# Two samples per count matmul: the second sample's one-hot rows scaled by 256, and the counts evicted as 16-bit integers

## The chip, the core and the metric

The kernel runs on one core of a Trainium2 chip. The metric is the device time of one execution in microseconds (us). Below, PE is TensorE's matmul unit, DVE is VectorE, ACT is ScalarE, POOL is GpSimd and SP is SyncE.

## What is computed

The reference is the forward pass of a recommender model for 16384 samples:

```
tok = word_emb[token_idx].mean(axis=1)      # 32 rows of 300, of 50000
e1, e2, e3 = mean of 20 rows each of emb_mh1, emb_mh2, emb_mh3   # rows of 64
o1..o4 = one row each of emb_oh1..emb_oh4
emb = concatenate([tok, e1, e2, e3, o1, o2, o3, o4], axis=1)     # 748 columns
wide = the same lookups, summed, in tables that are one column wide
h = relu(emb @ W1 + b1); h = relu(h @ W2 + b2); h = relu(h @ W3 + b3)
return sigmoid(h @ Wd + bd + wide)
```

W1 is 748 x 1024, W2 is 1024 x 512, W3 is 512 x 256.

## The kernel before

Samples are taken in 128 tiles of 128. Each tile has two kinds of lookups.

**Large table.** The 32 token rows of each sample are gathered from the chip's main memory: `tokens()` issues one indirect DMA on POOL's queue for each of the 32 index columns (L255), 128 rows of 1200 bytes each, two of them to a buffer `tok_rows`, with 8 buffers (`TOK_BUFS`). There are 4096 such gathers. DVE adds the rows up in `add_up` (L237, L239, L243). A gather waits until the adds have read its buffer.

**Small tables.** The seven small tables lie in SBUF as bf16, three terms that sum up to the f32 value (`terms`, made by `convert_tables`), cut into `n_h` = 138 slices of 128 rows. A lookup is made by counting: for each sample a 128 x 138 matrix says how often row l of slice h is asked for. `one_hots` (L314) compares the 64 lookup keys of each sample, which lie on 64 partitions, with an iota, and so makes `row1` (which of 128 rows) and `slice1` (which of 138 slices) in bf16; the upper 64 partitions hold the keys of a second sample. `counts` (L330) multiplies the two: one matmul over 64 partitions for each sample, with `f` choosing the lower or the upper half of the partitions, 12 matmuls of 64 x 138 for six pairs of samples, into a PSUM tile `pc` of four banks of which there is one. ACT evicts it into `cnt` as fp8, scaled by 0.5 (L347). One tile of samples takes 11 such steps (`STEPS`; the last has four pairs), so there are 1408 steps. During the next tile `small_sums` (L355) multiplies the counts, as weights (128 x 128, fp8), with the table terms (195 columns of bf16): 138 matmuls `pg` for each tile, and DVE reduces each pair of results (L371).

**Layers.** For two tiles at a time `mlp` runs the three layers in f32 (L461), each result evicted by ACT with Relu (L470) from one of two PSUM buffers `ph`.

**Order.** The order of all instructions is written out by the loop at L570 (`manual_schedule`). A step issues, in this order: the one-hots of the next step (DVE), the counts of this step (PE, then ACT), table conversions at the start of the run, transposes, token gathers and adds up to a share of the whole that grows evenly with the steps, the `pg` matmuls of this step, and layer matmuls up to an even share. The 16 last steps (`WAKE`) have no counts. Each engine takes its instructions in this order. Near the end `early_part` begins the last block's first layer in the tile of `pc`.

The line that matters for the layout of the counts is the eviction at L347: `cnt` is `[P, 2, HALF, n_h]`, so the 138 slices of a sample lie next to each other, and the weight load of `by_slice[:, :, h]` reads every 138th byte.

Of the kernel before, what the change touches and what calls it, by code (L numbers as in the profile page):

```python
# [11 lines left out]
I32 = mybir.dt.int32  # L12
U32 = mybir.dt.uint32
AF = mybir.ActivationFunctionType
ALU = mybir.AluOpType
AX = mybir.AxisListType

P = 128
# [10 lines left out]
LAYER_TILES = 2  # L29
HALF = P // 2  # L30
N_SMALL = 3 * N_MH + 4
ONEHOT = 6
# [19 lines left out]
def kernel(  # L52
# [46 lines left out]
    ps_h = ctx.enter_context(tc.tile_pool(name="ps_h", bufs=2, space=bass.MemoryType.PSUM))  # L99
    ps_c = ctx.enter_context(tc.tile_pool(name="ps_c", bufs=1, space=bass.MemoryType.PSUM))  # L100
    ps_g = ctx.enter_context(tc.tile_pool(name="ps_g", bufs=1, space=bass.MemoryType.PSUM))
# [45 lines left out]
    terms = const.tile([P, n_h, 3 * ROW], BF16, name="terms")  # L147
    minus_half = const.tile([P, P], BF16, name="minus_half")
    nc.vector.tensor_single_scalar(minus_half, ident, -0.5, op=ALU.mult)

# [16 lines left out]
    def convert_tables():  # L167
# [19 lines left out]
        def make(p, c):  # L187

            if c == 0:
                nc.scalar.activation(term(p, 0), rows(p), AF.Copy, scale=2.0)  # L190
                return
            _, a, b = pieces[p]
            left = ps_h.tile([P, SPLIT, ROW], F32, name="left", tag="ph")[:, 0 : b - a, :]
            nc.tensor.matmul(left, ident, rows(p), start=True, stop=False)  # L194
            for k in range(c):
                nc.tensor.matmul(left, minus_half, term(p, k), start=False, stop=(k == c - 1))
            nc.scalar.activation(term(p, c), left, AF.Copy, scale=2.0)

# [67 lines left out]
    def load_indices(blk):  # L266


        b0 = blk * BLOCK
        it = idxp.tile([P, NSUB, N_TOK], I32, name="it")  # L270
        nc.sync.dma_start(
            out=it, in_=idx[b0 : b0 + BLOCK, 0:N_TOK].rearrange("(s p) c -> p s c", p=P)
        )
        ix = keyp.tile([P, NSUB // 2, 2, N_SMALL], I32, name="ix")
        for s in range(NSUB):
            nc.sync.dma_start(
                out=ix[(s % 2) * HALF : (s % 2 + 1) * HALF, s // 2],
                in_=idx[b0 + s * P : b0 + (s + 1) * P, IDX_MH:IDX_COLS].rearrange(
                    "(f p) c -> p f c", p=HALF
                ),  # L280
            )
        token_indices[blk] = it
        return ix
# [30 lines left out]
    def one_hots(sc, s, i):  # L314
# [5 lines left out]
        for w, (one, n) in enumerate(((row1, P), (slice1, n_h))):  # L320
            shape = [P, rows, n // 2, 2]
            nc.vector.tensor_tensor(  # L322
                one[:, 0:rows, :].rearrange("p i (n d) -> p i n d", d=2),
                iota[:, 0:n].rearrange("p (n d) -> p n d", d=2).unsqueeze(1).to_broadcast(shape),
                sc[:, s // 2, w, s % 2, b : b + rows, :].unsqueeze(2).to_broadcast(shape),
                ALU.is_equal,
            )
        return row1, slice1

    def counts(cnt, hot, i):  # L330
# [3 lines left out]
        n = rows // 2  # L334
        pc = ps_c.tile([P, 2, 2, 512], F32, name="pc")
        for k in range(rows):
            for f in range(2):
                half = slice(f * HALF, (f + 1) * HALF)
                at = k % n * n_h
                nc.tensor.matmul(  # L340
                    pc[:, f, k // n, at : at + n_h],
                    hot[0][half, k, :],
                    hot[1][half, k, :],
                    start=True,
                    stop=True,
                )
        nc.scalar.activation(  # L347
            cnt[:, :, b : b + rows, :].rearrange("l f (g k) h -> l f g (k h)", g=2),
            pc[:, :, :, 0 : n * n_h],
            AF.Copy,  # L350
            scale=0.5,
            saturate=False,
        )

    def small_sums(g, cnt):  # L355


        by_slice = cnt.rearrange("l f p h -> l (f p) h")
        for i in (0, 2, 4, 6):
            pair = SMALL[i : i + 2]  # L360
            pg = ps_g.tile([P, 2, 3 * ROW], F32, name="pg")
            for j, f in enumerate(pair):
                h0, h1 = slices[f]
                for h in range(h0, h1):
                    nc.tensor.matmul(  # L365
                        pg[:, j, :], by_slice[:, :, h], terms[:, h, :], start=(h == h0), stop=(h == h1 - 1)
                    )
# [69 lines left out]
    def early_part(block):  # L437


        part = ps_c.tile([P, 4, 512], F32, name="pc")  # L440
        for m in range(4):
            for k in range(NK - 3):
                nc.tensor.matmul(
                    part[:, m, 0 : block.n],
                    w1_sb[: chunk_k[k], k, m * P : (m + 1) * P],
                    block.chunk(k),
                    start=(k == 0),
                    stop=False,
                )
        return part  # L450

    def layer(dst, weights, bias, srcs, n_out, part=None):

        n = srcs[0].shape[-1]
        for m in range(n_out):
            begun = part is not None and m < 4
            ph = part[:, m, :] if begun else ps_h.tile([P, N], F32, name="ph", tag="ph")
            for k, src in enumerate(srcs):
# [111 lines left out]
    for step in range(n_steps):  # L570
        t, i = divmod(step, STEPS)
        s = t % NSUB
        if i == 0:
# [7 lines left out]
            if t < tiles:  # L581
                if s == 0 and t:
                    sc = next_sc
                cnt = cp.tile([P, 2, HALF, n_h], FP8, name="cnt", tag="counts")
        if t < tiles:
# [78 lines left out]
```

## Time and profile before

| what | us |
|---|---|
| median of 3 runs | 7563.36 (7535.84 to 7567.44) |
| profiled execution: span from its first to its last instruction | 5191.3 |
| PE busy in the span | 5113.7 |
| DVE busy | 3890.9 |
| POOL busy | 3888.4 |
| ACT busy | 2600.7 |

For the profiled execution the page gives the span and no other time of its own: what lies around the span in it is not shown. The median of the runs is 2372 us more than the span. The granted TensorE clock over the span was 0.998.

The page lists busy time for each engine, the chain of work that ended last, and the groups of instructions by line, with the mean time of one and the idle time before it. A busy PE says little by itself: matmuls are pipelined and the recorded ends are modelled, so that the distance from one start to the next is what one matmul costs. POOL's recorded time of a gather is 949 ns, and the distance from one gather's start to the next is longer.

### The profile page before, as it was taken

To read this page: it belongs to the slowest core of one execution; us is meant where nothing else is said; L and a number is where in the kernel's file an instruction comes from. 1 tells how busy PE (TensorE), PEld (TensorE's weight loads), DVE (VectorE), ACT (ScalarE), POOL (GpSimd) and SP (SyncE) were. 2 spreads that over 40 slices of the span, in tenths; PEclk is the share of its full clock that TensorE was granted. 3 is DMA by queue.
4 is the path that set the end of the run, shared out by engine and by line. 5 is a ranking of instruction groups with operands and counts; after the bars stand their busy time and mean duration, and the time that the engine had idled before them with its cause. 6 is when DMAs were issued, how large, how long until landed. Compare 5 with 4: busy or idle time off the path is not lost.

```text
span 5191.3 us, 116518 instructions
## 1 busy us (share of the span) xinstructions
PE 5113.7 (99%) x46912; PEld 4177.5 (80%) x46912; DVE 3890.9 (75%) x8502; ACT 2600.7 (50%) x2445; POOL 3888.4 (75%) x4103
## 2 busy tenths in 40 slices
PE   7999999999999999999999999999999999999999
PEld 5888888888888888888888888888888878888888
DVE  6777777777777777777777777777777777777773
ACT  6555555555545545545445455555555545555552
POOL 7777777777777777777777777777777777777774
PEclk9999999999999999999999999999999999999999
DMA  7444444444444444444444444444444444444442
GB/s 201 123 126 125 125 126 124 125 126 125 126 124 126 125 126 125 126 124 126 125 126 126 124 126 125 126 126 123 125 125 126 125 126 124 126 125 126 124 124 77
DMA packets 253019, 653.38 MB, mean 126 GB/s; under 512 B 119056, under 2 KB 119633, under 8 KB 252477
## 3 DMA queue, kind: packets, MB, share of 16 engines
q0 software_dynamic: 196608, 629.41, 44.2%
q1 hardware_dynamic: 55869, 16.53, 1.4%
q8 instruction: 367, 6.01, 0.5%
q14 instruction: 175, 1.43, 0.1%
HBM read 645.59 MB, written 0.07 MB: 124 GB/s over the span
## 4 chain that ended last, share of the span: by engine, by line
PE 94%; DVE 2%; issue 1%; DMA 1%; ACT 0%; POOL 0%; SPq 0%; DVEq 0%; ACTq 0%
PE ph L461 46%; PE pg L365 32%; PE pc L340 12%; PE po L486 1%; PE pt L426 1%; PE pt L410 1%; PE pt L407 1%; DMA tok_rows<-in_word_emb_dram,it 1%; DVE own L239 1%; DVE own L243 0%; DMA w_sb<-in_W_dram 0%; POOL tok_rows L255 0%; DVE slice L322 0%; PE left L194 0%; PE pt L427 0%
## 5 line engine op out<-in xcount | busy, mean ns | idle before, releaser
L255 POOL DMA_INDIRECT tok_rows<-in_word_emb_dram,it x4096 | 3887.5, 949 | 1260.5 <-issue 873.6
L347 ACT ACTIVATE cnt<-pc 128x1656 fp8e3<-128x1656 f32 (+1 forms) x1408 | 2124.6, 1509 | 1607.7 <-PE pc L340 1592.1
L365 PE MATMUL pg<-terms,cnt 128*128 128x195 bf16 x17664 | 1828.7, 253 | 7.9 <-DVE g L371 7.6
L365 PEld LDWEIGHTS <-cnt 128*128 128x128 fp8e3 x17664 | 1590.3, 144 | 162.1 <-issue 31.8
L461 PE MATMUL ph<-h,w_sb 128*128 128x256 f32 (+1 forms) x5200 | 1224.2, 379 | 0.5 <-ACT h L470 0.5
L461 PE MATMUL ph<-x_small,w_sb 128*128 128x256 f32 (+2 forms) x4128 | 1044.4, 381 | 4.8 <-DVE x_small L429 3.0
L461 PEld LDWEIGHTS ph<-h,w_sb 128*128 128x128 f32 x5200 | 930.8, 191 | 99.2 <-issue 0.8
L322 DVE TENSOR_TENSOR row<-own,sc 128x768 bf16<-128x768 bf16 (+1 forms) x1408 | 762.3, 541 | 304.2 <-PE pc L340 251.5
L239 DVE TENSOR_TENSOR own<-own,tok_rows 128x300 f32<-128x300 f32 x1920 | 917.0, 478 | 63.3
L243 DVE TENSOR_TENSOR own<-own,tok_rows 128x300 f32<-128x300 f32 x1792 | 856.8, 478 | 61.8
L340 PEld LDWEIGHTS <-row 64*128 64x128 bf16 x16384 | 495.4, 94 | 484.8 <-issue 227.5
L470 ACT ACTIVATE h<-ph,b_sb 128x256 f32<-128x256 f32 (+1 forms) x906 | 426.8, 471 | 912.3 <-PE ph L461 912.0
L461 PEld LDWEIGHTS ph<-x_small,w_sb 128*128 128x128 f32 (+1 forms) x4128 | 739.3, 191 | 86.6 <-PE ph L461 6.4
L322 DVE TENSOR_TENSOR slice<-own,sc 128x828 bf16<-128x828 bf16 (+1 forms) x1408 | 795.5, 565 | 0.0
L340 PE MATMUL pc<-slice,row 64*128 64x138 bf16 x16384 | 751.0, 223 | 15.8 <-DVE slice L322 9.0
L461 PE MATMUL ph<-x_tok,w_sb 128*128 128x256 f32 (+1 forms) x2064 | 565.4, 380 | 0.0
L371 DVE TENSOR_REDUCE g<-pg 128x130 f32<-128x390 f32 (+1 forms) x512 | 261.1, 510 | 393.6 <-PE pg L365 391.0
L461 PEld LDWEIGHTS ph<-x_tok,w_sb 128*128 128x128 f32 x2064 | 373.0, 192 | 40.9
L428 DVE TENSOR_SCALAR x_tok<-pt 128x256 f32<-128x256 f32 x128 | 54.4, 425 | 301.6 <-PE pt L427 301.6
L411 DVE TENSOR_TENSOR x_small<-pt,scale 128x384 f32<-128x384 f32 x128 | 71.2, 556 | 91.8 <-PE pt L410 91.8
L486 PE MATMUL po<-h,wd_sb 128*1 128x256 f32 (+1 forms) x260 | 68.0, 374 | 1.6 <-DVE x_small L429 1.0
L490 DVE TENSOR_TENSOR h<-po,wide_row 1x256 f32<-1x256 f32 (+1 forms) x65 | 26.5, 408 | 54.9 <-PE po L486 51.9
(55 smaller groups left out, 872.4 us busy)
## 6 DMA issues: line engine op xcount, KB each, us to landing
tok_rows<-in_word_emb_dram,it POOLq DMA_INDIRECT x4096
ix<-in_idx_dram SPq DMA_DIRECT2D x128, 32.0 KB
w_sb<-in_W_dram SPq DMA_DIRECT2D x6, 512.0 KB
raw<-in_mh_dram SPq DMA_DIRECT2D x4, 682.5 KB
it<-in_idx_dram SPq DMA_DIRECT2D x32, 64.0 KB
w_sb<-in_W_dram SPq DMA_DIRECT2D x1, 2048.0 KB
out_dram<-h SPq DMA_DIRECT2D x63, 1.0 KB
raw<-in_mh_dram SPq DMA_DIRECT2D x2, 227.5 KB
```

The costliest lines, as they stand in the source:

```text
L239: nc.vector.tensor_add(tok_sum, tok_sum, a)
L243: nc.vector.tensor_add(to, tok_sum, b)
L255: nc.gpsimd.indirect_dma_start(out=rows[:, r * TOK_D : (r + 1) * TOK_D], out_offset=None, in_=word, in_offset=bass.IndirectOffsetOnAxis(ap ...
L322: nc.vector.tensor_tensor(one[:, 0:rows, :].rearrange("p i (n d) -> p i n d", d=2), iota[:, 0:n].rearrange("p (n d) -> p n d", d=2).unsque ...
L340: nc.tensor.matmul(pc[:, f, k // n, at : at + n_h], hot[0][half, k, :], hot[1][half, k, :], start=True, stop=True,)
L347: nc.scalar.activation(cnt[:, :, b : b + rows, :].rearrange("l f (g k) h -> l f g (k h)", g=2), pc[:, :, :, 0 : n * n_h], AF.Copy, scale=0 ...
L365: nc.tensor.matmul(pg[:, j, :], by_slice[:, :, h], terms[:, h, :], start=(h == h0), stop=(h == h1 - 1))
L371: nc.vector.tensor_reduce(g[:, at : at + n * ROW].rearrange("p (f d) -> p f d", f=n), pg[:, 0:n, :].rearrange("p f (c d) -> p f d c", c=3) ...
L411: nc.vector.tensor_tensor(self.small[:, 0:3, at], pt[:, 0:3, :], scale.unsqueeze(2).to_broadcast([P, 3, P]), ALU.mult)
L461: nc.tensor.matmul(ph[:, 0:n], weights[: src.shape[0], k, m * P : (m + 1) * P], src, start=(k == 0), stop=(k == len(srcs) - 1),)
L470: nc.scalar.activation(dst[:, m, 0:n], ph[:, 0:n], AF.Relu, bias=bias[:, m : m + 1])
L486: nc.tensor.matmul(po[:, 0:n], wd_sb[:, k : k + 1], h3[:, k, 0:n], start=(k == 0), stop=(k == M3 - 1))
```

## The change

The two samples of a pair are counted in one matmul over all 128 partitions. For this the upper half of `row1` is multiplied by 256 by a new ACT instruction in place, so that the sum is count(first) + 256 x count(second). ACT evicts it without a scale as a 16-bit integer, and the two bytes of that integer are then read as two fp8 numbers: byte n as fp8e3 has the value n/64 for the counts that occur, and the table terms are scaled by 64 instead of 2. The key DMAs put neighbouring samples (2p, 2p+1) into one pair, so that the bytes come out in the order of the samples. `cnt` is now `[P, n_h, HALF]` of 16-bit integers: the samples of one slice lie next to each other, the weight load reads 128 neighbouring bytes, and the eviction writes 2-byte elements 128 bytes apart. The PSUM tile `pc` has two banks instead of four, and there are two of them. `early_part` takes its four banks from two such tiles.

```
-    ps_c = ctx.enter_context(tc.tile_pool(name="ps_c", bufs=1, space=bass.MemoryType.PSUM))
+    ps_c = ctx.enter_context(tc.tile_pool(name="ps_c", bufs=2, space=bass.MemoryType.PSUM))
...
-    minus_half = const.tile([P, P], BF16, name="minus_half")
-    nc.vector.tensor_single_scalar(minus_half, ident, -0.5, op=ALU.mult)
+    minus_count = const.tile([P, P], BF16, name="minus_count")
+    nc.vector.tensor_single_scalar(minus_count, ident, -1.0 / COUNT, op=ALU.mult)
...
-                nc.scalar.activation(term(p, 0), rows(p), AF.Copy, scale=2.0)
+                nc.scalar.activation(term(p, 0), rows(p), AF.Copy, scale=COUNT)
...
-                    "(f p) c -> p f c", p=HALF
+                    "(p f) c -> p f c", f=2
...
+        upper = row1[HALF:P, 0:rows, :]
+        nc.scalar.activation(upper, upper, AF.Copy, scale=UPPER)
         return row1, slice1
...
-        pc = ps_c.tile([P, 2, 2, 512], F32, name="pc")
+        pc = ps_c.tile([P, 2, 512], F32, name="pc")
         for k in range(rows):
-            for f in range(2):
-                half = slice(f * HALF, (f + 1) * HALF)
-                at = k % n * n_h
-                nc.tensor.matmul(
-                    pc[:, f, k // n, at : at + n_h],
-                    hot[0][half, k, :],
-                    hot[1][half, k, :],
-                    start=True,
-                    stop=True,
-                )
+            at = k % n * n_h
+            nc.tensor.matmul(
+                pc[:, k // n, at : at + n_h], hot[0][:, k, :], hot[1][:, k, :], start=True, stop=True
+            )
         nc.scalar.activation(
-            cnt[:, :, b : b + rows, :].rearrange("l f (g k) h -> l f g (k h)", g=2),
-            pc[:, :, :, 0 : n * n_h],
+            cnt[:, :, b : b + rows].rearrange("l h (g k) -> l g k h", g=2),
+            pc[:, :, 0 : n * n_h].rearrange("l g (k h) -> l g k h", h=n_h),
             AF.Copy,
-            scale=0.5,
-            saturate=False,
         )
...
-        by_slice = cnt.rearrange("l f p h -> l (f p) h")
+        by_slice = cnt.bitcast(FP8)
...
-                        pg[:, j, :], by_slice[:, :, h], terms[:, h, :], start=(h == h0), stop=(h == h1 - 1)
+                        pg[:, j, :], by_slice[:, h, :], terms[:, h, :], start=(h == h0), stop=(h == h1 - 1)
...
-                cnt = cp.tile([P, 2, HALF, n_h], FP8, name="cnt", tag="counts")
+                cnt = cp.tile([P, n_h, HALF], U16, name="cnt", tag="counts")
```

Here `UPPER` is 256, `COUNT` is 64, `HALF` is 64 and `U16` is a 16-bit unsigned integer. The order of the instructions on PE, DVE, POOL and SP is otherwise the same; on ACT the scaling of the next step's rows stands ahead of this step's eviction.

More of the change, by code (lines that the diff above doesn't have):

```diff
@@ L13 @@
 U32 = mybir.dt.uint32
+U16 = mybir.dt.uint16
 AF = mybir.ActivationFunctionType
@@ L30 @@
 HALF = P // 2
+UPPER = 256.0
+COUNT = 64.0
 N_SMALL = 3 * N_MH + 4
@@ L195, in make @@
             for k in range(c):
-                nc.tensor.matmul(left, minus_half, term(p, k), start=False, stop=(k == c - 1))
-            nc.scalar.activation(term(p, c), left, AF.Copy, scale=2.0)
+                nc.tensor.matmul(left, minus_count, term(p, k), start=False, stop=(k == c - 1))
+            nc.scalar.activation(term(p, c), left, AF.Copy, scale=COUNT)
         for step in range(len(pieces) + 2):
@@ L437, in early_part @@
     def early_part(block):
[L440 to L449, printed above, removed]
+        part = []
+        for pair in range(2):
+            two = ps_c.tile([P, 2, 512], F32, name="pc")
+            for m in range(2):
+                part.append(two[:, m, :])
+                for k in range(NK - 3):
+                    nc.tensor.matmul(
+                        part[-1][:, 0 : block.n],
+                        w1_sb[: chunk_k[k], k, (2 * pair + m) * P : (2 * pair + m + 1) * P],
+                        block.chunk(k),
+                        start=(k == 0),
+                        stop=False,
+                    )
         return part
@@ L456, in layer @@
             begun = part is not None and m < 4
-            ph = part[:, m, :] if begun else ps_h.tile([P, N], F32, name="ph", tag="ph")
+            ph = part[m] if begun else ps_h.tile([P, N], F32, name="ph", tag="ph")
             for k, src in enumerate(srcs):
```

## The prediction

> **What bounds the kernel now.** I read the busy line of the page first, then the groups.
>
> ```profile
> PE 5113.7 (99%) x46912; PEld 4177.5 (80%) x46912; DVE 3890.9 (75%) x8502; ACT 2600.7 (50%) x2445; POOL 3888.4 (75%) x4103
> ```
> ```profile
> L255 POOL DMA_INDIRECT tok_rows<-in_word_emb_dram,it x4096 | 3887.5, 949 | 1260.5 <-issue 873.6
> L347 ACT ACTIVATE cnt<-pc 128x1656 fp8e3<-128x1656 f32 (+1 forms) x1408 | 2124.6, 1509 | 1607.7 <-PE pc L340 1592.1
> L340 PE MATMUL pc<-slice,row 64*128 64x138 bf16 x16384 | 751.0, 223 | 15.8 <-DVE slice L322 9.0
> ```
>
> PE seems to be the bound at 99%. But POOL's row hides a second one: 3887.5 us busy and 1260.5 us idle before its gathers make 5148.0 us of the 5191.3. That idle time comes in equal pieces. In the order of time, at the very start, when PE has done nothing that POOL could wait for:
>
> ```profile
> 4.51 0.94 POOL L255 DMA_INDIRECT tok_rows<-in_word_emb_dram,it  x1 [0.30 <-issue]
> 5.76 0.95 POOL L255 DMA_INDIRECT tok_rows<-in_word_emb_dram,it  x1 [0.30 <-issue]
> 7.02 0.95 POOL L255 DMA_INDIRECT tok_rows<-in_word_emb_dram,it  x1 [0.30 <-issue]
> 8.27 0.94 POOL L255 DMA_INDIRECT tok_rows<-in_word_emb_dram,it  x1 [0.30 <-issue]
> ```
>
> and in the middle of the run:
>
> ```profile
> 2503.63 0.94 POOL L255 DMA_INDIRECT tok_rows<-in_word_emb_dram,it  x1 [0.30 <-issue]
> 2504.88 0.95 POOL L255 DMA_INDIRECT tok_rows<-in_word_emb_dram,it  x1 [0.31 <-issue]
> 2506.13 0.94 POOL L255 DMA_INDIRECT tok_rows<-in_word_emb_dram,it  x1 [0.30 <-issue]
> 2507.38 0.95 POOL L255 DMA_INDIRECT tok_rows<-in_word_emb_dram,it  x1 [0.30 <-DVE own L243]
> ```
>
> A gather starts every 1.25 us in both places. This is POOL's own pace, not a wait for buffers that a slow PE would cause. 4096 x 1.2526 us = 5131 us, and with 3.1 us before the first gather and the work after the last one this is the span. So the profiled execution has two engines at their limit, and only one of them is touched.
>
> PE's own cost must be read from starts:
>
> ```profile
> 2497.93 1.48 PE L461 MATMUL ph<-h,w_sb 128*128 128x256 f32 x6
> 2499.35 0.54 PE L340 MATMUL pc<-slice,row 64*128 64x138 bf16 x12
> 2499.82 1.52 PE L365 MATMUL pg<-terms,cnt 128*128 128x195 bf16 x15
> ```
>
> Twelve count matmuls take 0.47 us from the first start to the start of `pg`. The six f32 records ahead of them take 1.42 us, where their usual distance of 0.216 us (the commonest in the trace) makes 1.30: about 0.1 us is lost on entering. The starts over the whole run give 0.311 us from the last `ph` record to the first `pc` (0.095 over 0.216), 0.327 us for eleven distances within a group of twelve, and 0.152 us from the last `pc` to `pg`. That is 0.57 us for one step, 1408 x 0.57 = 0.81 ms for the run.
>
> Only near the end does PE hold POOL up:
>
> ```profile
> 5131.31 0.42 DVE L428 TENSOR_SCALAR x_tok<-pt 128x256 f32<-128x256 f32 x1 [16.10 <-PE pt L427]
> ...
> 5134.82 0.95 POOL L255 DMA_INDIRECT tok_rows<-in_word_emb_dram,it  x1 [7.75 <-DVE own L243]
> ```
>
> DVE waits 16.10 us for PE's transpose, the token adds queue behind it, and the gather waits 7.75 us for its buffer.
>
> **What the Trainium skill says.** "TensorEngine Tiling (Array Packing)", Key Properties, says that a change of the tiling mode drains TensorE. The trace agrees: about 0.095 us more where PE goes from 128 rows to 64, and 0.152 us instead of about 0.06 on the way back. "ScalarE: Activation LUTs", What ACT_TABLE_LOAD costs, prices an ACTIVATE with immediate operands at 186 ns + 0.833 ns for each element: 1565 ns for 1656 elements, and the trace has 1551. "Advanced Engine Details and Errata", SBUF Cachelines, says that going to another 16-byte line with every access costs extra, without saying how much. The trace of before has no ACT write of that kind.
>
> **The change part by part.** *Count matmuls.* A step has 6 matmuls of 128 rows instead of 12 of 64, and as many weight loads. The nearest row is the key transposes (L305: bf16, 128 columns, a weight load each), which start 0.056 us apart; `pg` with 195 columns goes at 0.087. In between, 138 columns give 0.056 + 10 x (0.031/67) = 0.061 us. Six make 0.37 us. The neighbours also use 128 rows, so both drains go. 0.57 - 0.37 = 0.20 us, x 1408 = 0.28 ms less PE work: 5.19 becomes 4.91 ms. If the entry cost were one of f32 to bf16 and stayed, 0.10 us would be left, 0.15 ms in all. Either way PE falls below POOL's 5131 us, and more than 5191 - 5131 = 60 us cannot come out of it.
>
> *Weight loads of `pg`.* They read neighbouring bytes now. Their matmuls already start 0.083 to 0.088 us apart; I take 0 of gain. From below, a gain up to 0.004 us x 17664 = 0.07 ms of PE, again covered by POOL. A loss is excluded, since the bytes, type and count stay and only the step gets shorter.
>
> *Two `pc` buffers.* Counts no longer wait for the eviction. That wait was 6.8 us in 7 cases in the profile: nothing.
>
> *Eviction.* 828 elements instead of 1656. With strided writes free it is 186 + 0.833 x 828 = 0.88 us; if every element takes double, 1.57 us, as long as before (1.55). I take the latter, because the page on cachelines expects a penalty. Total 1.24 to 2.15 ms against 2.12.
>
> *Scaling the upper half.* 1408 new ACT instructions, SBUF to SBUF, 64 partitions x 768 (512 in the last step of a tile). The nearest row is L190, 577 ns for 455 elements; with 313 more at 0.833 it is 0.84 us, and 1280 x 0.84 + 128 x 0.62 = 1.15 ms. ACT's other work is 0.48 ms. ACT's sum is 2.87 to 3.78 ms, 55 to 73% of the span: off the path.
>
> *The new wait.* ACT's scaling of step k+1 waits for DVE's `row`, and behind it queue the eviction of step k and the Relu of step k (0.47 us, which frees `ph` for PE). DVE makes that row a step ahead: in the trace it starts as soon as the earlier count group has left its buffer, together with the eviction. PE waits for the scaled row 0.56 + 0.84 us after the row began instead of 1.13 us for both one-hots, and there is a whole step of 3.64 us for it. With a second `ph` buffer and a second `pc` I cost it at 0; with that cover gone it would be 0.3 us a step, 0.4 ms. POOL's queue and SP's are not passed by anything; the key DMAs are as many, of the same 256-byte rows.
>
> *Table terms.* Only constants change: 0.
>
> *What is late next.* POOL. The last gather started at 5148.6 us. Two stalls near the end (3.2 and 8.7 us between starts instead of 1.25) are PE's backlog: 9.4 us. After the last gather 13.7 us pass until the last token add starts, because the adds are backed up; with PE in time some 4 would do. I take half of that, 5 us. The last tile's layers (28.5 us) stay. Sum: 5191 - 14 = 5177 us of span.
>
> **The profiled time and the median.** The page shows only the span of 5191 us for the profiled execution; the median is 2372 us above it, and nothing on the page says where. If it lies around the span, it stays. If the whole execution is slower in timed runs by 1.457, 14 us become 20. Both give 7563 - 14 to 20, say 7550.
>
> **The rivals.** *B: PE is the bound of the timed runs.* If the missing 2372 us are PE's, POOL has room, and PE's saving counts: 0.28 of 5.19 ms is 5.5%, 7563 x 0.945 = 7150 us. For it: the chain of waits puts 94% on PE. Against it: the granted clock is 0.998 and nothing shows PE slower. *C: ACT becomes the bound, slower.* The place is the strided eviction. ACT's other work per step is 0.82 + 0.34 = 1.16 us, so it decides once the eviction is over 3.64 - 1.16 = 2.5 us, about 2.8 times the contiguous price per element. At four times it is 0.186 + 4 x 0.69 = 2.95 us, a step is 4.11 us, and 1408 steps make 5.79 ms, 0.6 ms more: 8160 us. For it: a line per element, untried here. Against it: half speed would leave 27% of ACT free. A milder form, ACT's head-of-queue waits, would end between 7563 and this. *That the change doesn't do what it says* is possible only in PE's drains, if they stay; the forecast is the same, since POOL hides it.
>
> **How the numbers follow.** Forecast (POOL bounds) 0.56, B 0.24, C 0.20. The forecast's own range is 7525 to 7590 us. To leave out no more than 2 in 10, I go down to 7120, over most of B (the rest would be a still larger gain), and up to 7640, over the mildest part of C. About 0.5% (38 us) is what a measurement can tell from no change. Faster: 0.24 from B and 0.02 from the forecast's lower end; same 0.53; slower: 0.20 from C and 0.01.
>
> **What would show it right or wrong.** Right: gathers still 1.25 us apart, PE's busy share visibly lower, with waits for DVE's one-hots or ACT's scaling in front of the counts, six `pc` matmuls some 0.06 us apart, no jump on entering, a span near 5177 us. The eviction's mean tells C: below 2.5 us it can't bound. B is right if the span hardly moves and the time falls by hundreds of us. The forecast is wrong if gathers start closer together than 1.25 us, or if POOL waits for adds all along.

## The result, and the profile after

The changed kernel takes 7871.04 us (median of 4 runs, 7866.36 to 7876.35); the kernel before, beside it, 7562.81 us (4 runs, 7535.84 to 7567.44). The ratio is 1.0415 with an interval of 1.0393 to 1.0437: slower by 4%, and outside the range that was given. The profiled execution of the changed kernel took 7867.21 us, with a span of 7865.4 us: here nothing lies around the span.

The kernel before took 7536 to 7712 us in some sessions and 5191 to 5196 us in others, even on one and the same chip, and since the profile shown ahead of the prediction (span 5191.3 us) is of the second kind and the result of the first, each experiment is compared with runs of the kernel before that were made beside it.

The page of the changed kernel, busy line and chain:

```profile
PE 5731.0 (73%) x38720; PEld 4626.8 (59%) x38720; DVE 3894.7 (50%) x8502; ACT 6954.3 (88%) x3853; POOL 3876.0 (49%) x4103
...
ACT 72%; PE 15%; another core or an unknown queue 5%; issue 5%; DVE 2%; ACTq 0%; DVEq 0%; SPq 0%; DMA 0%
ACT cnt L346 56%; ACT row L332 11%; PE ph L461 7%; PE pg L362 5%; ACT h L470 4%; PE pc L343 2%; DVE own L242 1%; DVE own L246 0%; DVE slice L325 0%; DVE row L325 0%; PE po L486 0%; PE left L197 0%; ACT h L491 0%; PE pt L423 0%
```

ACT went from 2600.7 us (50%) to 6954.3 us (88%) and now holds 72% of the chain. The kernel before, in a session like this one (e0 below), has ACT at 2575.6 us and at 5% of the chain. The groups, lines of the same page (busy us, mean ns of one | idle before):

```profile
L258 POOL DMA_INDIRECT tok_rows<-in_word_emb_dram,it x4096 | 3875.1, 946 | 3946.1 <-DVE own L246 2605.5
L346 ACT ACTIVATE cnt<-pc 128x828 uint16<-128x828 f32 (+1 forms) x1408 | 5308.1, 3770 | 389.2 <-remote 164.6
L343 PE MATMUL pc<-slice,row 128*128 128x138 bf16 x8192 | 812.0, 235 | 836.8 <-ACT row L332 510.8
L332 ACT ACTIVATE row<-row 64x768 bf16<-64x768 bf16 (+1 forms) x1408 | 1154.9, 820 | 77.1 <-DVE row L325 39.9
```

The eviction was 1509 ns on the mean for 1656 or 1104 elements; it is 3770 ns for 828 or 552. That is 5308.1 - 2124.6 = 3184 us more, and the scaling adds 1154.9 us: together 4338 us of the 4354 us that ACT grew. PE's counts wait 510.8 us for the scaled rows. POOL waits 2605.5 us for the token adds; that is hardly the change's doing, since it waits 2435.4 us for them in the kernel before too, in a session like this one (e0).

The groups of the same kernel, each shape apart, price an element:

```profile
L346 ACT ACTIVATE cnt<-pc 128x828 uint16<-128x828 f32 x1280 | 4971.3, 3884 | 384.3 <-remote 164.2 <-PE pc L343 141.0 <-PE ph L461 32.0
L346 ACT ACTIVATE cnt<-pc 128x552 uint16<-128x552 f32 x128 | 336.8, 2631 | 4.9 <-PE pc L343 1.4 <-remote 0.4
```

(3884 - 2631) / 276 = 4.54 ns an element, where the contiguous outputs further below cost 0.83 ns.

ACT in the order of time, in the middle of the run of the changed kernel (start us, us):

```profile
3998.54 0.84 ACT L332 ACTIVATE row<-row 64x768 bf16<-64x768 bf16 x1
3999.41 3.90 ACT L346 ACTIVATE cnt<-pc 128x828 uint16<-128x828 f32 x1
4003.33 0.84 ACT L332 ACTIVATE row<-row 64x768 bf16<-64x768 bf16 x1
4004.19 3.90 ACT L346 ACTIVATE cnt<-pc 128x828 uint16<-128x828 f32 x1
4008.11 0.47 ACT L470 ACTIVATE h<-ph,b_sb 128x256 f32<-128x256 f32 x1
```

ACT hardly rests here: the scaling of the next step, the eviction of this one and the Relu stand end to end, some 0.03 us apart. A pair of scaling and eviction takes 4.79 us from start to start. PE in the same stretch waits in front of every group of counts:

```profile
4004.23 0.54 PE L343 MATMUL pc<-slice,row 128*128 128x138 bf16 x6 [1.20 <-ACT cnt L346]
4004.61 1.37 PE L362 MATMUL pg<-terms,cnt 128*128 128x195 bf16 x14
...
4009.51 0.54 PE L343 MATMUL pc<-slice,row 128*128 128x138 bf16 x6 [1.77 <-ACT row L332]
```

### The profile page after: what moved, and what is told of

The parts are those of the page before. It is cut to its first block, busy times and chain, and to the rows that moved or that the text cites. A ratio compares the mean times of both kernels' runs of the same rounds, so it can differ in the third digit from the quotient of the medians.

```text
span 7865.4 us, 102784 instructions
## 1 busy us (share of the span) xinstructions
PE 5731.0 (73%) x38720; PEld 4626.8 (59%) x38720; DVE 3894.7 (50%) x8502; ACT 6954.3 (88%) x3853; POOL 3876.0 (49%) x4103
## 4 chain that ended last, share of the span: by engine, by line
ACT 72%; PE 15%; another core or an unknown queue 5%; issue 5%; DVE 2%; ACTq 0%; DVEq 0%; SPq 0%; DMA 0%
ACT cnt L346 56%; ACT row L332 11%; PE ph L461 7%; PE pg L362 5%; ACT h L470 4%; PE pc L343 2%; DVE own L242 1%; DVE own L246 0%; DVE slice L325 0%; DVE row L325 0%; PE po L486 0%; PE left L197 0%; ACT h L491 0%; PE pt L423 0%
## 5 line engine op out<-in xcount | busy, mean ns | idle before, releaser
L258 POOL DMA_INDIRECT tok_rows<-in_word_emb_dram,it x4096 | 3875.1, 946 | 3946.1 <-DVE own L246 2605.5
L346 ACT ACTIVATE cnt<-pc 128x828 uint16<-128x828 f32 (+1 forms) x1408 | 5308.1, 3770 | 389.2 <-remote 164.6
L362 PE MATMUL pg<-terms,cnt 128*128 128x195 bf16 x17664 | 2065.6, 268 | 436.5 <-issue 327.2
L362 PEld LDWEIGHTS <-cnt 128*128 128x128 fp8e3 x17664 | 1675.4, 106 | 598.6 <-issue 471.0
L461 PE MATMUL ph<-h,w_sb 128*128 128x256 f32 (+1 forms) x5200 | 1398.4, 412 | 190.5 <-ACT h L470 111.3
L343 PE MATMUL pc<-slice,row 128*128 128x138 bf16 x8192 | 812.0, 235 | 836.8 <-ACT row L332 510.8
L461 PE MATMUL ph<-x_small,w_sb 128*128 128x256 f32 (+2 forms) x4128 | 1219.1, 427 | 224.8 <-ACT h L470 138.7
L343 PEld LDWEIGHTS <-row 128*128 128x128 bf16 x8192 | 603.6, 103 | 1258.8 <-ACT row L332 706.3
L461 PEld LDWEIGHTS ph<-h,w_sb 128*128 128x128 f32 x5200 | 1014.0, 209 | 389.9 <-ACT h L470 130.8
L332 ACT ACTIVATE row<-row 64x768 bf16<-64x768 bf16 (+1 forms) x1408 | 1154.9, 820 | 77.1 <-DVE row L325 39.9
L461 PEld LDWEIGHTS ph<-x_small,w_sb 128*128 128x128 f32 (+1 forms) x4128 | 832.5, 217 | 391.1 <-ACT h L470 161.5
```

The source lines that it names most:

```text
L258: nc.gpsimd.indirect_dma_start(out=rows[:, r * TOK_D : (r + 1) * TOK_D], out_offset=None, in_=word, in_offset=bass.IndirectOffsetOnAxis(ap ...
L332: nc.scalar.activation(upper, upper, AF.Copy, scale=UPPER)
L343: nc.tensor.matmul(pc[:, k // n, at : at + n_h], hot[0][:, k, :], hot[1][:, k, :], start=True, stop=True)
L346: nc.scalar.activation(cnt[:, :, b : b + rows].rearrange("l h (g k) -> l g k h", g=2), pc[:, :, 0 : n * n_h].rearrange("l g (k h) -> l g k ...
L362: nc.tensor.matmul(pg[:, j, :], by_slice[:, h, :], terms[:, h, :], start=(h == h0), stop=(h == h1 - 1))
L461: nc.tensor.matmul(ph[:, 0:n], weights[: src.shape[0], k, m * P : (m + 1) * P], src, start=(k == 0), stop=(k == len(srcs) - 1),)
```

## The experiments

The theory after the result was rival C: the eviction writes 2-byte elements 128 bytes apart, each of them costs 4.5 ns, and ACT becomes the bound. Against it stood: the scaling and its place in ACT's order make the difference; the second PSUM buffer does; the weight loads of `pg` do. And two questions were left from the prediction: why the median stood 2372 us over the profiled span, and whether POOL or PE bounds the kernel before.

### The kernel before, once more: e0_before_again

No edit. 

> The kernel before, unchanged, for a second profile. In the changed kernel's profiled execution the span (7865.4 us) and the time (7867.2 us) are 2 us apart; in the profile of the kernel before, the span was 5191.3 us and the median 7563. Theory 1: the execution that was profiled before is not like the ones that were timed; a second profile has a span near 7560 us, and shows which engine carries the extra 2370 us. Theory 2: the two differ by something around the span; then the span is 5191 us again and the time 7563.

Measured: 7666.4 us, span 7664.3 us; the kernel before in the runs beside it 7681.84 us (7667.84 to 7712.43, 7 runs). So the 2.4 ms lie inside the span. Its page, and below it PE in the order of time, with the idle time ahead of each group in brackets, and ACT's next eviction ("remote" is a signal whose sender the profile does not show):

```profile
PE 6024.2 (79%) x46912; PEld 4723.0 (62%) x46912; DVE 3889.4 (51%) x8502; ACT 2575.6 (34%) x2445; POOL 3877.3 (51%) x4103
```
```profile
3990.19 0.54 PE L340 MATMUL pc<-slice,row 64*128 64x138 bf16 x12
...
3992.39 0.37 PE L365 MATMUL pg<-terms,cnt 128*128 128x195 bf16 x2 [0.50 <-issue]
3993.82 0.46 PE L365 MATMUL pg<-terms,cnt 128*128 128x195 bf16 x3 [1.07 <-issue]
3995.23 0.32 PE L365 MATMUL pg<-terms,cnt 128*128 128x195 bf16 x1 [0.94 <-issue]
...
4001.01 1.55 ACT L347 ACTIVATE cnt<-pc 128x1656 fp8e3<-128x1656 f32 x1 [3.81 <-remote]
```

In the middle of `pg`, with weights and terms in SBUF, PE stops for 0.5 to 1.1 us and nothing in the profile holds it. Idle times of PE of more than 0.44 us that the profile puts down to "issue" number 534 in this run, 484 us together or 0.9 us each (two expectations below say 0.7); the first profile has none.

But the stops of PE are not all. ACT's eviction at 4001.01 us takes the counts whose matmuls are recorded from 3990.19 to 3990.73 us: it starts 10 us later, though ACT was free from 3997.20 us on. Over the run 468 of the 1408 evictions start more than 1 us after both ACT is free and the last recorded end of their matmuls, 1743 us of delay together; in the first profile the longest such delay is 0.1 us. The ends of matmuls are modelled, so this doesn't tell whether PE finished late or its signal came late, and part of PE's further idle time is spent waiting for ACT and DVE, which were themselves kept waiting.

PE's busy time is 6024.2 - 5113.7 = 910 us longer too. The granted clock is 0.873 on the mean instead of 0.998, and half speed for 26% of the time: 310 of the 311 stretches at half speed have idle time of PE in the 6.8 us ahead of them (twice the shortest stretch), against two thirds of moments taken at random. POOL waits 2435.4 us for the adds, so it is not the bound in sessions of this kind; these readings point to PE and to how late the others are released by it.

### The eviction made contiguous: e1_contiguous

The counts are laid out as before (138 slices of a pair next to each other), as 16-bit integers. Its output is not the reference's: the weight load reads other bytes, as many as before and 138 apart.

```
-            cnt[:, :, b : b + rows].rearrange("l h (g k) -> l g k h", g=2),
-            pc[:, :, 0 : n * n_h].rearrange("l g (k h) -> l g k h", h=n_h),
+            cnt[:, b : b + rows, :].rearrange("l (g k) h -> l g (k h)", g=2),
+            pc[:, :, 0 : n * n_h],
...
-        by_slice = cnt.bitcast(FP8)
+        by_slice = cnt.bitcast(FP8).rearrange("l p w -> l (p w)").rearrange("l (q h) -> l q h", h=n_h)
...
-                        pg[:, j, :], by_slice[:, h, :], ...
+                        pg[:, j, :], by_slice[:, :, h], ...
...
-                cnt = cp.tile([P, n_h, HALF], U16, name="cnt", tag="counts")
+                cnt = cp.tile([P, HALF, n_h], U16, name="cnt", tag="counts")
```

> The changed kernel with one part undone: the eviction writes its 16-bit integers next to each other (sample by sample), everything else as in the change. The weight load then can't read the two samples' bytes with one step, so it reads 128 other bytes, 138 bytes apart as in the kernel before; the output is not the reference's. Theory 1 (the strided write makes ScalarE the bound): the eviction falls from 3.77 us to about 0.86 us, ScalarE's sum from 6.95 to about 2.85 ms, and the time falls below the kernel before, to 5200 us if nothing but the gathers' own pace is left, or stays near 7560 us if what holds the kernel before at 7563 us holds here too. Theory 2 (the new scaling on ScalarE, between the one-hots and the counts, makes the waits): the eviction gets shorter, but the time stays over 7700 us.

Measured: 7324.35 us against 7681.84 us, a ratio of 0.9517 (0.9487 to 0.9547). The eviction's row in its page:

```profile
L346 ACT ACTIVATE cnt<-pc 128x828 uint16<-128x828 f32 (+1 forms) x1408 | 1181.7, 839 | 1738.7 <-remote 872.7
```

839 ns instead of 3770. Scaling, its place and both PSUM buffers are still there, and the kernel is faster than before: what makes the change slow is the pattern of the eviction's writes.

### Six neighbours written together: e2_runs_of_six

Memory, layout and weight loads stay as in the change; only the order in which ACT walks through the same elements is another. The six samples of a slice, 12 neighbouring bytes, are written one after another, and it is the read from PSUM that strides (552 bytes between samples).

```
-            cnt[:, :, b : b + rows].rearrange("l h (g k) -> l g k h", g=2),
-            pc[:, :, 0 : n * n_h].rearrange("l g (k h) -> l g k h", h=n_h),
+            cnt[:, :, b : b + rows].rearrange("l h (g k) -> l h g k", g=2),
+            pc[:, :, 0 : n * n_h].rearrange("l g (k h) -> l h g k", h=n_h),
```

> The changed kernel with the eviction's order turned: the same elements go to the same places, but the six samples of a slice, which are 12 neighbouring bytes, are written one after another, and PSUM is read with a step of 138 elements. If each jump to another place in SBUF costs some 3.7 ns (4.54 less 0.83), the eviction is about 0.17 + 828 x 0.83 + 138 x 3.7 ns = 1.37 us, and the time is that of contiguous writes or near it. If every 2-byte element costs its 4.5 ns by its size, not by the jump, the eviction stays at 3.8 us and the time at 7870 us. If the strided read of PSUM costs as much as the write did, likewise.

Measured: 7319.1 us against 7681.84 us, 0.9516 (0.9483 to 0.955), the same as e1. Its page:

```profile
PE 5704.6 (78%) x38720; PEld 4663.6 (64%) x38720; DVE 3881.5 (53%) x8502; ACT 2839.7 (39%) x3853; POOL 3880.4 (53%) x4103
...
L346 ACT ACTIVATE cnt<-pc 128x828 uint16<-128x828 f32 (+1 forms) x1408 | 1190.0, 845 | 1706.6 <-remote 926.5
```

The number of elements, their bytes and the addresses are those of the change, and 845 ns is the contiguous price. So it isn't the step of 128 bytes in itself; it is that successive writes don't meet. The expectation's 1.37 us for a cost at every jump was too high. The strided read from PSUM costs nothing that shows. e1 and e2 still differ from the kernel before in the second `pc` buffer and in a shorter eviction, besides the halved matmuls; which of these brings the 4.8% was not run.

### What a write costs: m1_evictions

A kernel that only evicts: 828 f32 elements of PSUM a partition, eight times each with another type and distance of the output. It computes nothing of the reference.

```
t = sb.tile([P, 828, step], dtype, name=name)
for _ in range(REPEAT):
    nc.scalar.activation(t[:, :, 0].rearrange("p (g k) -> p g k", g=2), flat, AF.Copy, saturate=False)
```

> Not the model: only ScalarE copies of 828 f32 elements from PSUM to SBUF, 8 of each form, and 8 by VectorE; the output is a constant. Forms: fp8, 16-bit integers at steps of 1, 2, 4, 8 and 64 elements, bf16 at 1 and 16, f32 at 1, 4, 8 and 16. Theory 1 (a write that goes to another line with each element is slow): about 0.86 us at step 1 for all types, rising with the step in bytes to 3.88 us at 128 bytes; at equal steps in bytes f32 is like 16 bit. Rival: only elements narrower than 4 bytes are slow when strided, and f32 stays at 0.86 us at any step. Rival: the conversion to integers is slow at any step. VectorE in the changed kernel's form: between 0.95 and 3.9 us.

Measured, ns of one: the commonest of eight, since the first of a group can be up to 0.33 us longer. Distances are from the start of one element to the start of the next:

| output | contiguous | 4 bytes apart | 8 | 16 | 32 | 64 | 128 |
|---|---|---|---|---|---|---|---|
| fp8 | 860 | | | | | | |
| 2-byte | 860 | 1087 | 1999 | 3827 | 3622 (bf16) | | 3850 |
| f32 | 860 | | | 1619 | 1648 | 1550 | |

Some of its groups and stretches, the last with seven instructions in one line:

```profile
L44 ACT ACTIVATE u_rows<-src 128x828 uint16<-128x828 f32 x8 | 30.8, 3855 | 0.2
L54 DVE CAST u_dve<-src 128x828 uint16<-128x828 f32 x8 | 30.7, 3836 | 182.4 <-ACT f_rows L49 182.1
L29 ACT ACTIVATE f_s<-src 128x828 fp8e3<-128x828 f32 x8 | 6.9, 860 | 0.2
```
```profile
44.68 26.98 ACT L29 ACTIVATE u_s<-src 128x828 uint16<-128x828 f32 x7
```

The change's eviction takes 3855 ns with nothing beside it, so contention can have no more than 1% of its 3884. VectorE pays the same (3836), so moving the eviction there would save nothing. The cost of 2-byte writes goes in proportion to the 16-byte lines that are touched: 207, 414 and 828 lines at distances of 4, 8 and 16 bytes; (3827 - 1999) / 414 = 4.42 ns a line, which leaves 1999 - 414 x 4.42 = 169 ns for the instruction, and 169 + 4.42 x 207 = 1084 against 1087 measured. Beyond 16 bytes it no longer grows (3622 to 3850). A lone f32 costs (1619 - 169) / 828 = 1.75 ns: a full 4-byte word is cheaper than half a word. The Trainium skill, "Advanced Engine Details and Errata", SBUF Cachelines, names 16-byte lines and a dependence on the type without sizes; these runs agree with both and give the sizes. No theory of the expectation held as it was put: f32 at the same distance is neither like 2-byte types nor free.

### Without the scaling: e3_strided_no_scaling, e4_six_no_scaling

The change and e2, each without the scaling, in sessions where the kernel before takes 5193.86 us. The output isn't the reference's: the second sample of each pair is not scaled.

```
-        upper = row1[HALF:P, 0:rows, :]
-        nc.scalar.activation(upper, upper, AF.Copy, scale=UPPER)
```

> The changed kernel without ScalarE's scaling of the upper half (so both samples' counts are added into one byte; the output is not the reference's), the strided eviction as in the change. Theory 1 (ScalarE's sum is the bound): 1155 us of its 6954 us go, and the time falls by 400 us or more, down to the 7320 us that the kernel with cheap evictions has. Theory 2 (what matters is that the scaling stands between the one-hots and the counts and ahead of the eviction in ScalarE's order): the time falls too, and to the same; what tells them apart is the next run.

Measured: 5758.36 us against 5193.86 us (5190.79 to 5195.75, 21 runs), 1.1082 (1.1064 to 1.1101). Its page:

```profile
PE 5051.9 (88%) x38720; PEld 4356.3 (76%) x38720; DVE 3895.4 (68%) x8502; ACT 5410.2 (94%) x2445; POOL 3878.5 (67%) x4103
```

The eviction alone puts ACT at 94% and the kernel above the one before. The time is 1496 us below that of the whole change in such a session (7254.13 us, e7 below), which is more than the 1155 us that the scaling takes. ACT in the order of time shows more of it:

```profile
2997.01 7.64 ACT L344 ACTIVATE cnt<-pc 128x828 uint16<-128x828 f32 x2
3004.10 0.75 ACT L468 ACTIVATE h<-ph,b_sb 128x256 f32<-128x256 f32 x1
3004.72 3.91 ACT L344 ACTIVATE cnt<-pc 128x828 uint16<-128x828 f32 x1
```

The Relu starts at 3004.10 us, 0.55 us before the evictions ahead of it end (2997.01 + 7.64), and so does nearly every instruction behind an eviction here. With the scaling in the program nearly each starts some 0.03 us after the one before it has ended (e7's lines below). Why the scaling keeps them apart isn't shown. So the eviction alone makes the change slower here, and the scaling adds to it because ACT is full. Whether the change without its scaling is slower than the kernel before in a session like the result's was not run; what was run there (e1, e2) says that the change with its scaling is faster once the eviction is cheap.

> The kernel with runs of six (7319 us) without the scaling of the upper half (the output is not the reference's). Theory 1: with a cheap eviction ScalarE has 60% of its time free, the scaling is off the path, and the time stays within 0.5% of 7320 us. Theory 2: the new hop through ScalarE costs wherever it stands; the time falls by 1% or more.

Measured: 5178.66 us, 0.997 (0.9957 to 0.9982), ACT at 1648.0 us (32%). With a cheap eviction the kernel without the scaling gains 0.3%; e8 below, with it, gains 0.5% in another session of this kind. The scaling costs no time here, with ACT at 55% (e8) and the gathers as the bound. Both expectations had named 7320 us for a session of the other kind; there e4 was not run.

### One count buffer: e5_six_one_buffer

e2 with one `pc` buffer instead of two (`early_part` takes its two tiles under two names).

```
-    ps_c = ctx.enter_context(tc.tile_pool(name="ps_c", bufs=2, space=bass.MemoryType.PSUM))
+    ps_c = ctx.enter_context(tc.tile_pool(name="ps_c", bufs=1, space=bass.MemoryType.PSUM))
...
-            two = ps_c.tile([P, 2, 512], F32, name="pc")
+            two = ps_c.tile([P, 2, 512], F32, name="pc", tag=("pc", "pc_late")[pair])
```

> The kernel with runs of six, with one count buffer in PSUM instead of two. If the gain of 360 us over the kernel before comes from the second buffer (in the second profile of the kernel before, TensorE's counts wait 365 us for the eviction), it goes: near 7600 us. If it comes from half the count matmuls and the drains that are gone, it stays near 7320 us, less what the wait for an eviction of 0.85 us instead of 1.55 us is.

Measured: 5180.32 us against 5193.86 us, 0.9973 (0.9962 to 0.9984); with two buffers it is 0.9953 (0.9939 to 0.9967, e8 below), and the intervals overlap. The second buffer is worth at most some 0.2% here. But the gathers bound both kernels, and the expectation was about a session in which PE does: PE's counts wait 87.7 us for evictions with one buffer, which POOL covers here. How much of e2's 4.8% the second buffer brings stays open.

### The kernel before without gathers: e6_before_no_gathers, e10_no_gathers_again

The adds read one constant buffer; the output isn't the reference's, since no token row is looked up. POOL and the gathers' transfers are gone, all else is there.

```
+    fixed_rows = tokp.tile([P, TOK_GROUP * TOK_D], F32, name="fixed_rows")
+    nc.vector.memset(fixed_rows, 1.0)
...
-                rows = tokp.tile([P, TOK_GROUP * TOK_D], F32, name="tok_rows")
-                for r in range(TOK_GROUP):
-                    j = q * TOK_GROUP + r
-                    nc.gpsimd.indirect_dma_start(...)
+                rows = fixed_rows
```

> The kernel before without the token gathers: GpSimd issues none, and VectorE adds the same constant rows instead (the output is not the reference's). In the second profile of the kernel before TensorE stands still for 0.7 us at a time with nothing to wait for in the profile, in some 200 episodes of 4 to 10 us, and its clock is at half in a quarter of the time; the first profile had neither. If the gathers' traffic makes these stops, they go, and the span is TensorE's own 5190 us or less. If they come from TensorE itself, they stay and the time is 6500 us or more.

Measured: 5194.45 us against 5193.86 us, 1.0 (0.999 to 1.0009), PE busy 5113.8 us (98%). PE by itself needs as long as PE and POOL together, and the gathers at their own pace need 5131 us: the kernel before has two bounds of nearly one height.

The same kernel was then run in a session in which the kernel before takes 7563.25 us (7550.83 to 7564.66, 3 runs).

> The kernel before without the token gathers, again (the output is not the reference's), because the session of its first run was one in which the kernel before takes 5194 us, where TensorE doesn't stop anyway. In a session in which the kernel before takes 7550 us: if the gathers' traffic makes TensorE stop for 0.7 us at a time, the time is near 5190 us; if TensorE stops by itself, or for its own instructions, it stays over 6500 us. In a session of 5194 us it is 5194 us again and tells nothing new.

Measured: 5194.64 us, 0.6872 (0.6852 to 0.6892). Its page:

```profile
PE 5114.7 (99%) x46912; PEld 4177.8 (80%) x46912; DVE 3890.7 (75%) x8503; ACT 2603.6 (50%) x2445; POOL 0.9 (0%) x7
```

Without gathers PE has neither stops nor a lower clock (0.998 granted), in a session where the kernel with them takes 2.37 ms longer. So the stops are an effect of the gathers or their transfers. Which of the two, how they reach PE and why only some sessions have it was not found.

### The change where PE doesn't stop: e7_after_again

The changed kernel, unedited, in a session where the kernel before takes 5194.23 us.

> The changed kernel itself, again. The last four kernels ran on a chip where the kernel before takes 5194 us, as in its first profile, and not 7563 us, and there the changed kernel without its scaling took 5758 us, which is ScalarE's sum of work in it. If this chip is like that one, theory 1 (ScalarE's sum is the bound) gives the changed kernel's ScalarE work of 6954 us and some 20 to 50 us around it: 6970 to 7010 us, 1.34 to 1.35 times the kernel before. If the hop through ScalarE costs waits too (theory 2), it is over 7100 us. On a chip like the first one: 7870 us again, 1.04 times.

Measured: 7254.13 us (7251.06 to 7255.71), 1.3965 (1.3943 to 1.3987). Its page and ACT in the order of time:

```profile
PE 5350.0 (74%) x38720; PEld 4447.1 (61%) x38720; DVE 3904.4 (54%) x8502; ACT 6958.5 (96%) x3853; POOL 3878.2 (53%) x4103
...
L346 ACT ACTIVATE cnt<-pc 128x828 uint16<-128x828 f32 (+1 forms) x1408 | 5312.7, 3773 | 60.4 <-PE pc L343 26.8
```
```profile
2996.57 3.89 ACT L346 ACTIVATE cnt<-pc 128x828 uint16<-128x828 f32 x1
3000.49 0.84 ACT L332 ACTIVATE row<-row 64x768 bf16<-64x768 bf16 x1
3001.35 3.89 ACT L346 ACTIVATE cnt<-pc 128x828 uint16<-128x828 f32 x1
```

ACT works 96% of the span. That I expected about 250 us less was an omission. ACT is idle for 292 us: 90 us are the 0.02 to 0.03 us between neighbours (3000.49 against 2996.57 + 3.89), and 202 us lie in 176 longer waits, most of them for PE's layer results and for DVE's rows. By the expectation's own words a time over 7100 us speaks for theory 2, waits that the hop through ACT brings. In part it is right: beside ACT's sum there are these waits, and the overlap that e3 has and this run lacks. PE's clock is 0.928 here without any gathers' stops: 215 of its 216 stretches at half speed have idle time of PE in the 6.8 us ahead of them (five sixths of random moments do), here mostly waits for ACT.

Where the kernel before takes 5194 us the change costs 2060 us, in the session of the result 308 us. The two delays seem to overlap there, since PE would have to wait for ACT at many of the times when it stops by itself; that is a reading of the two numbers, not tested apart.

### The two cures once more: e8_six_again, e9_contiguous_again

e2 and e1, unedited, beside e7.

> The kernel with runs of six (two count buffers), again. Where the kernel before takes 5194 us: 5180 us as with one buffer (ratio 0.997), since the gathers' own pace of 1.25 us x 4096 = 5131 us leaves no more. Where the kernel before takes 7560 to 7680 us: 7320 us (ratio 0.95).

> The changed kernel with contiguous evictions (its weight load reads other bytes, so the output is not the reference's), again, for the same chip as the two kernels beside it. The eviction costs 0.84 us in both, so the same time as with runs of six within 0.5%.

Measured against 5194.23 us: e8 5169.71 us (5167.68 to 5170.59), 0.9953 (0.9939 to 0.9967); e9 5171.21 us, 0.9956 (0.994 to 0.9972). Both are alike although e8's weight loads read neighbouring bytes and e9's every 138th, and so are e2 and e1 (7319.1 and 7324.35 us) where the gathers are not the bound: that rearrangement is worth nothing that shows. The page of e8, and its gathers in the order of time:

```profile
PE 4830.1 (94%) x38720; PEld 4247.5 (82%) x38720; DVE 3850.8 (75%) x8502; ACT 2840.7 (55%) x3853; POOL 3877.4 (75%) x4103
...
L258 POOL DMA_INDIRECT tok_rows<-in_word_emb_dram,it x4096 | 3876.5, 946 | 1250.9 <-issue 756.3
```
```profile
3000.96 0.95 POOL L258 DMA_INDIRECT tok_rows<-in_word_emb_dram,it  x1 [0.30 <-DVE own L246]
3002.21 0.95 POOL L258 DMA_INDIRECT tok_rows<-in_word_emb_dram,it  x1 [0.30 <-issue]
3003.47 0.95 POOL L258 DMA_INDIRECT tok_rows<-in_word_emb_dram,it  x1 [0.30 <-DVE own L246]
```

PE needs 5113.7 - 4830.1 = 284 us less and the kernel gets 24.5 us faster: the gathers, 1.25 us apart as ever, are the bound that is left. This is the change as the prediction had it, and it needs one reordered pattern.

### How long a run must be: m2_runs

828 elements in runs of 1, 2, 3 and 6 neighbours, the runs 128 bytes apart; it computes nothing of the reference.

```
t = sb.tile([P, 828 // count, 128 // mybir.dt.size(dtype)], dtype, name=name, tag="t")
...
dst = t[:, :, 0:count].rearrange("p (g n) k -> p g n k", g=2)
```

> Not the model: ScalarE copies of 828 f32 elements from PSUM to SBUF, written in runs of 1, 2, 3 or 6 neighbouring 16-bit integers (half) or 1 or 3 f32 (word), the runs 128 bytes apart, and 16-bit runs of 1 and 6 on VectorE; the output is a constant. With runs of six the eviction took 0.845 us in the model, no more than contiguous. If the jump to another place costs 3.7 ns and hides behind the elements of a run that follow, a run of n costs the larger of 4.5 ns and n x 0.83 ns: 3.85 us for runs of one, 1.95 for two, 1.35 for three, 0.86 for six. If what costs is a write that doesn't fill 4 bytes, runs of two are as fast as one f32: 1.6 us for half the jumps of one f32's, about 0.86 us. VectorE likewise.

Measured, the groups with each shape apart (names: half is a 2-byte type on ACT, word is f32 on ACT, vec is a 2-byte type on DVE, then the length of the run):

```profile
L32 ACT ACTIVATE half_one<-src 128x828 uint16<-128x828 f32 x8 | 30.8, 3850 | 0.2
...
L32 ACT ACTIVATE word_one<-src 128x828 f32<-128x828 f32 x8 | 12.4, 1551 | 0.3
L32 ACT ACTIVATE half_three<-src 128x828 uint16<-128x828 f32 x8 | 11.2, 1398 | 0.3
L34 DVE CAST vec_six<-src 128x828 uint16<-128x828 f32 x8 | 8.2, 1020 | 0.3
L32 ACT ACTIVATE half_two<-src 128x828 uint16<-128x828 f32 x8 | 6.9, 862 | 0.3
```

Two neighbours, one full 4-byte word, are enough: 862 ns. Three, with a third element alone in its word, cost more than two: 1398 ns, as 276 lines at 4.42 ns do (169 + 276 x 4.42 = 1389). What fits all these runs is that the costly thing is a line in which a 4-byte word is left partly written. All runs began at a multiple of 4 bytes, so two elements that straddle two words were not tried. The skill's "Advanced Engine Details and Errata", SBUF Cachelines, asks for at least two hits on a line to absorb the latency. Runs of two agree (862 ns), but 2-byte elements 8 bytes apart hit each line twice and take 1999 ns, and runs of three hit it three times and take 1398: two hits are not enough here, and the measurement decides.

## Why the prediction was wrong

**The step that failed: "Eviction".** It set 828 elements between 0.88 us, strided writes free, and 1.57 us, every element double, and took 1.57. Measured: 3.88 us, 4.54 ns for an element instead of 1.67. The upper end was the fault: the skill's section gave no size, the trace of before had no such write, and nothing excluded more than double. The prediction knew that above 2.5 us the sign turns, and put that at 0.20 against "half speed would leave 27% of ACT free", which argues from the value it had chosen. The result is rival C's mechanism and place: e1 and e2 change the write pattern, with the scaling and both buffers in place, and the slowdown is gone; e3 keeps the pattern without the scaling and is still slower than the kernel before, in its own session. (The lower total of 1.24 ms was a slip: it takes all 1408 evictions as 828 elements, and with the 128 shorter ones it is 1.20 ms.)

**Rival C's size was wrong too, twice.** Its eviction of 2.95 us was too cheap, and its 8160 us added ACT's extra 0.6 ms to the 7563 us. A new bound takes the place of the old one and hides most of its delays: 1408 steps of ACT's work take 7254 us (e7) where PE doesn't stop by itself, and 617 us more where it does, against 2.37 ms more for the kernel before.

**"The profiled time and the median" failed as well.** The 2372 us do not lie around the span, nor are they a uniform slowing; they are stops, late releases and a lower clock of PE within the span (e0), which vanish with the gathers (e10). Rival B had the better bound for the sessions in which the result was taken: with the eviction cured the change gains 4.8% there (e2: 0.9516; B said 5.5%). That the sizes are so near is partly luck, since B scaled PE's saving by the whole time and put the second `pc` buffer at nothing, where e0's counts wait 365.3 us for the eviction.

**Right, in the sum of the others:**

- *Count matmuls*: starts in e8, whose counts are those of the change, mostly lie 0.059 to 0.064 us apart, 0.216 us behind the last `ph` matmul (the usual distance) and 0.063 us ahead of `pg`: 0.37 us a step as forecast. Both drains went, although f32 still changes to bf16 there, which agrees with the skill's "TensorEngine Tiling (Array Packing)", Key Properties. PE's busy time falls by 284 us (e8) against 0.28 ms.
- *Scaling*: 840 ns and 626 ns, 1154.9 us in all, against 0.84, 0.62 and 1.15 ms. Its price came from an ACT row, and the price in the skill's "ScalarE: Activation LUTs", What ACT_TABLE_LOAD costs, fits the contiguous outputs here within 2% (an estimate of 826 ns for 768 elements against 840, 876 for 828 against 860). That it also breaks the overlap of ACT's instructions (e3) was not foreseen.
- *Weight loads of `pg`*: nothing (e8 against e9, e2 against e1). *Two `pc` buffers*: next to nothing where the gathers are the bound (e5); not measured where they are not.
- *POOL's pace is the next bound*: shown by e8, with 24.5 us of gain in time in a session without stops where 14 us were forecast. The traces tell it apart: the two stalls near the end shrink from 9.4 us to one of 1.5 us, all stalls together by 11 us, and between the other gathers lie 1.2505 us on the mean instead of 1.2529, some 10 us in all, which nothing had forecast. The remaining 5 us of the span's 25.5 came from another place than the forecast's: 13.7 us still pass between the last gather and the last token add (so they were not a backlog), and it is the time after that add that fell from 29.0 to 24.3 us.
- *The new wait*: 0 was right with a cheap eviction where the gathers are the bound (e4 beside e8: 36.4 us of PE's waits are for scaled rows in e8). With the dear one PE waits 510.8 us for them; as ACT is full there, this is ACT's bound seen from PE and not a cost of its own.

## What to carry to other kernels

Let two successive elements of a 2-byte output fill one 4-byte word, by the order in which the pattern is walked if the layout is given; the input side of this eviction from PSUM took the stride for nothing (845 ns, e2). When a cost has no row in the profile and no size anywhere, ask at what value the sign of the answer turns, and give what lies beyond it the weight that ignorance deserves, rather than choosing double. And when the median stands far from the profiled span, the profile is of another regime than the one timed: the bound has to be argued for both.

## What the runs showed of the hardware

- Writes of 2-byte elements into SBUF that leave 4-byte words partly written fit a cost of 4.2 to 4.4 ns for each 16-byte line they fall into (828 lone elements 16 bytes or more apart: 3622 to 3850 ns on ACT; 3837 on DVE, where only runs of one and six were tried; contiguous 860 on ACT). A line in which only whole words are written costs 1.7 to 1.8 ns if each element has a new one (f32, 16 bytes or more apart: 1550 to 1648), and nothing over the 0.83 ns per element in runs of three (862).
- Reading PSUM with a stride of 552 bytes within the eviction was free (845 ns, e2).
- ACT's instructions overlapped by some 0.5 us behind a strided eviction (e3) and hardly ever once the scaling stood in the program (e7): 1496 us of difference for 1155 us of scaling. The reason stays open.
- In some sessions the gathers make PE stop some 0.9 us at a time, and what waits for PE is released up to 10 us after the recorded end of its matmuls: 7563 us against 5195 us without gathers (e10). In other sessions the same kernel with gathers takes 5194 us. What tells the sessions apart stays open.
- Nearly every stretch at half speed of PE's clock had idle time of PE in the 6.8 us ahead of it, by such stops (e0, 310 of 311) and by waits for ACT (e7, 215 of 216), each time more often than random moments (two thirds and five sixths).
